# A graph kernel's second pass: four chunks by lists where three were, and where the dense entries, the own columns and the last product go

## The chip, the cores and the metric

The kernel runs on one core of a Trainium2 chip. The metric is the device time of one execution in microseconds (us). It was timed in 14 runs; the median counts.

## What is computed

A graph of 3327 nodes with 512 features goes through two layers. Both use the same sparse weighted adjacency matrix `adj`, given as a dense array. The density falls with the node number: the first nodes are neighbours of many, the last of few. Cut to what matters:

```python
# layer 0
h = maximum(layernorm(x), 0)
u = relu(adj @ (h @ W1) + b1)              # first pass over adj, 128 hidden features (u here is g in the kernel)
x = x + adj @ (u @ W2) + b2                # second pass over adj
# layer 1
h = maximum(layernorm(x), 0)
type_sum = adj @ h
attn_a = sigmoid([type_sum, h] @ Wa.T + ba); attn_b = sigmoid([type_sum, h] @ Wb.T + bb)
s = h @ W_sa;  scores = (s @ a_left)[:, None] + (s @ a_right)[None, :]
e = where(adj != 0, exp(-leaky_relu(scores, 0.01)), 0)
x_a = (e / (e.sum(1) + 1e-5)) @ s
x_b = adj @ (h @ W_gcnb) + b_gcnb
x = x + sigmoid(attn_a * x_a + attn_b * x_b)
```

## The kernel before

The nodes are padded to 3328, 26 blocks of 128 (`NB`). Chunks are four blocks wide (512 columns), the last to be visited two. `adjT` is the transposed adjacency matrix in DRAM. Five engines work side by side: TensorE (PE), VectorE (DVE), ScalarE (ACT), GpSimd (POOL) and SyncE (SP); each runs its own instructions in order, and SP, ACT and POOL also issue DMAs in that order.

**First pass** (lines 603 to 651). The loop `for n, c in enumerate(back)` visits the chunks from the last nodes to the first (`back`: columns 2816, 2304, 1792, 1280, 256, 768, 0). For each of the 26 row blocks j it multiplies u[j] by a 128x512 piece of `adjT` (L622), and DVE takes the largest magnitude of every group of 32 columns (L629, tile `most`). The loads of two row blocks each (512 KB, `load_adj`, L301) go through SP's queue into six buffers. From `most`, `make_lists` (L482) finds for each block of nodes and each pair of 32-node groups which rows have a nonzero in the group, and writes row numbers to `row_h` and `row_a`. The room for such a list is `list_rooms(NB)`: 8 entries of 64 rows each for block 1, falling to 3, and 2 for some. Where a block stands in `OWN`, its own columns are left out of the lists and kept dense; where it also stands in `TOP`, the first 64 nodes are too. `extra[i]` counts these dense entries (0, 1 or 2).

The tile `ae[i]` holds for block i the `adjT` pieces of all its entries, listed or dense. Listed pieces come by indirect DMAs of POOL, one for 128 rows, in the order of `gather_adj` (L187): some behind the matmuls of the first pass, some in the second, the rest in attention. Dense pieces come by `load_own` (L210): two loads of 64 rows per entry (16 KB each). They are issued on ACT from n = 2 on, at j = 6, 10, 16, 19 and 22, one block each time, and each waits for the matmul of that step (`pace`). ACT's queue also carries the loads of the hub columns `a_hub` and of weights (L334 to L347).

**Second pass** (lines 693 to 966). Of the seven chunks the first three of `back` (`LISTED = 3`, blocks 14 to 25) are summed by lists: POOL gathers rows of g from DRAM (`gather_g`, 68 of them, a ring of 24), and `list_sums` (L865) multiplies them by `ae` pieces of 64x32 (L882). The dense entries use g itself, or `g_top`, a copy of the first 64 rows of g (L908 to L913). The chunk's sums are copied by ACT, turned by PE (L897) and copied again. The other chunks (blocks 0 to 13: three of 512 columns, one of 256) are summed densely by `dense_sums` (L916), which reads `adjT` again (L925). What PE does when is written out in `PLAN`: `d` is one step of a dense sum, `s` one block of list sums, `t` the turn of a listed chunk, `x` a row block of layer 0's output and its normalization (`make_row`: L723 on PE, then DVE and ACT, a store to `h_dram`), `l` the turn of left scores, `h` one addition to the hub's sums (L775), `e` a block of hub scores on DVE and ACT. `MADE` is the order in which dense (d) and listed (l) chunks are finished. Every 1.4 us of estimated work (`SPACE`, `STEP`) POOL issues one gather, of g as long as the ring has room, otherwise the next of `gather_adj`.

"Hub" is block 0, whose 128 nodes have the most neighbours. It is summed densely: 26 additions of `a_hub` and 26 of `e_hub`. What PLAN leaves of them is done after the last row.

**Attention** (lines 1032 to 1330). Blocks 25 down to 1, each with `rooms + extra` entries, cut into segments of four or five at most. For each segment `attend` gathers the rows of h that the lists name (POOL, tiles `rows` and `hr`) and makes the scores; `sums` multiplies (L1135: eight instructions per entry); two blocks later `turn` and `weigh` multiply the sums by the weights (L1149, L1189, L1197) and `finish` makes the output. Dense entries use `h_own`, loaded for each block, or `h_top`, a copy of the first 64 rows of h in the memory of `a_hub`. After each block `fetch_ae` issues two more gathers of `ae`; what a block still lacks is fetched before its h rows. `LEAD` holds POOL back: the gathers of block i wait for the sums of block i+4 (i+3 for the first).

At the end block 1's product `p_a` is made in two column pieces in one PSUM bank, `cuts = (0, WH, D)`, so that the work on the first may begin early.

## Time and profile before

| | us |
|---|---|
| median of 14 runs | 792.63 |
| lowest and highest | 787.24 and 800.37 |
| the profiled execution | 791.12 |
| its span, first to last instruction | 789.4 |
| end of the first pass, first dense matmul of the second | 230.6 |
| last row's matmul (px) ends | 400.6 |
| POOL's first gather of h rows | 413.65 |
| attention's PE work without larger gaps from | 446.9 |
| last p_a matmul ends | 780.0 |

The page gives busy time by engine, forty slices, the DMA queues, the chain of work that ended last, and groups of instructions with count, busy time, mean duration and the idle time ahead of them. Times on timelines count from the span's start. A matmul of float32 is two PE instructions. Matmul records overlap, so the time of one comes from the distance between starts or from the group's busy time, not from its mean. "issue" is time in which the engine waited for nothing that the profile shows.

| queue or issue | count | size |
|---|---|---|
| a<-in_adjT_dram, SP | 129 | 512 KB |
| ae<-in_adjT_dram, ACT (own columns) | 52 | 16 KB |
| ae gathers, POOL | 178 | one of 128 rows |
| g_row gathers, POOL | 68 | |
| h row gathers, POOL (rows, hr) | 178 | |

### The profile page before, as it was taken

What the parts mean: (1) busy time and instruction counts of PE and PEld (TensorE: products, weight loads), DVE (VectorE), ACT (ScalarE), POOL (GpSimd) and SP (SyncE); (2) the same over time, 40 slices, a digit from 0 to 9 for tenths busy, and PEclk for the clock granted to TensorE, in tenths of its full rate; (3) what the DMA queues carried; (4) which work ended last, traced back from release to release, by engine and by line L of the source; (5) the groups of instructions that cost most, each with busy time, mean ns of one, the idle gap of its engine ahead of it and who ended that gap; (6) DMA issues with size and microseconds to landing.
All of it is one profiled execution on the core that took longest, in us unless ns stands there. A gap on an engine that the chain in (4) does not pass through costs nothing.

```text
span 789.4 us, 11919 instructions
## 1 busy us (share of the span) xinstructions
PE 715.9 (91%) x3715; PEld 389.2 (49%) x3715; DVE 484.3 (61%) x1530; ACT 204.7 (26%) x492; POOL 456.1 (58%) x487
## 2 busy tenths in 40 slices
PE   9999959998889989898797399889999999999994
PEld 7775424444454444344444165445555545555553
DVE  6777958889961337456282277347657475766552
ACT  7771000000000324445170123123132222222211
POOL 2400566766766767677607667776767776675300
PEclk9999979999999999999988799989999999999998
DMA  8789959999869999974249566756666777786500
GB/s 277 245 302 302 298 171 311 296 282 284 269 202 299 366 371 344 320 248 148 61 181 307 151 179 205 231 156 189 213 196 191 211 213 229 227 252 199 159 32 31
DMA packets 105738, 180.47 MB, mean 229 GB/s; under 512 B 21217, under 2 KB 38017, under 8 KB 105666
## 3 DMA queue, kind: packets, MB, share of 16 engines
q1 hardware_dynamic: 63632, 111.91, 42.0%
q0 software_dynamic: 22112, 54.46, 24.3%
q10 hardware_dynamic: 19922, 13.25, 5.4%
q8 instruction: 31, 0.51, 0.3%
q14 instruction: 41, 0.34, 0.1%
HBM read 157.64 MB, written 22.26 MB: 228 GB/s over the span
## 4 chain that ended last, share of the span: by engine, by line
PE 73%; issue 9%; DVE 5%; POOL 4%; DMA 3%; another core or an unknown queue 3%; ACT 1%; SPq 0%; ACTq 0%; POOLq 0%
PE acc_u L622 16%; PE acc L1135 11%; PE p_b L1189 10%; PE acc_g L925 9%; PE p_a L1197 9%; PE acc_hub L775 5%; PE px L723 3%; PE pu L380 3%; PE ptt L1149 2%; POOL hr L180 2%; DVE most L629 2%; PE acc_s L882 1%; PE pt L372 1%; POOL ae L180 1%
## 5 line engine op out<-in xcount | busy, mean ns | idle before, releaser
L180 POOL DMA_INDIRECT ae<-in_adjT_dram,row_a x178 | 186.1, 1046 | 130.3 <-DVE jb L578 57.4
L622 PE MATMUL acc_u<-a,rows 128*128 128x512 f32 (+1 forms) x364 | 160.2, 581 | 2.7 <-issue 2.7
L180 POOL DMA_INDIRECT hr<-h_rows,row_h x114 | 118.5, 1039 | 51.9 <-issue 28.0
L1189 PE MATMUL p_b<-W_g_sb,tyT 128*128 128x257 f32 x416 | 100.9, 391 | 10.4 <-issue 9.5
L629 DVE TENSOR_REDUCE most<-a 128x32 f32<-128x1024 f32 (+1 forms) x104 | 103.7, 1009 | 10.4 <-DMA a<-in_adjT_dram 6.8
L180 POOL DMA_INDIRECT rows<-h_rows,row_h x64 | 67.5, 1055 | 55.8 <-DVE es_hub L830 21.3
L1189 PEld LDWEIGHTS p_b<-W_g_sb,tyT 128*128 128x128 f32 x416 | 77.6, 192 | 43.1 <-issue 18.7
L622 PEld LDWEIGHTS acc_u<-a,rows 128*128 128x128 f32 x364 | 68.0, 197 | 61.7 <-issue 59.1
L1197 PE MATMUL p_a<-W_sa_sb,tyT 128*128 128x512 f32 (+2 forms) x216 | 94.4, 577 | 1.1 <-issue 1.0
L180 POOL DMA_INDIRECT g_row<-g_rows,row_h x68 | 71.6, 1053 | 29.9 <-issue 18.0
L925 PE MATMUL acc_g<-a,g 128*128 128x512 f32 (+1 forms) x208 | 85.3, 552 | 1.1 <-DMA a<-in_adjT_dram 1.1
L1164 DVE COPY tyT<-ptt 128x512 f32<-128x512 f32 x51 | 35.0, 686 | 69.4 <-PE ptt L1149 44.3
L1197 PEld LDWEIGHTS p_a<-W_sa_sb,tyT 128*128 128x128 f32 x216 | 40.6, 189 | 40.5 <-issue 38.7
L925 PEld LDWEIGHTS acc_g<-a,g 128*128 128x128 f32 x208 | 39.1, 194 | 39.3 <-issue 36.2
L1135 PE MATMUL acc<-hr,ae 64*64 64x512 f32 x456 | 54.7, 592 | 0.3 <-issue 0.3
L727 DVE SCALAR_TENSOR_TENSOR xb<-px,xb 128x512 f32<-128x512 f32 x26 | 17.9, 687 | 50.3 <-PE px L723 40.9
L390 ACT ACTIVATE gT<-acc_u,b_col 128x512 f32<-128x512 f32 (+1 forms) x7 | 4.6, 656 | 163.1 <-DMA ae<-in_adjT_dram 89.4
L988 DVE SCALAR_TENSOR_TENSOR a_hub<-h_own,w_own 128x512 f32<-128x512 f32 x52 | 35.5, 683 | 9.1 <-DMA rows<-h_rows,row_h 9.0
L278 DVE SCALAR_TENSOR_TENSOR ae<-ae 128x192 f32<-128x192 f32 (+2 forms) x31 | 12.2, 404 | 41.8 <-ACT ae L277 24.3
L1071 ACT COPY s_left<-pl 64x64 f32<-64x64 f32 x42 | 8.7, 206 | 106.7 <-PE pl L1067 52.6
L1135 PEld LDWEIGHTS acc<-hr,ae 64*64 64x64 f32 x456 | 19.1, 135 | 30.3 <-issue 28.8
L1149 PEld LDWEIGHTS ptt<-ident,ty 128*128 128x128 f32 x208 | 24.9, 144 | 18.0 <-issue 12.9
(166 smaller groups left out, 994.5 us busy)
## 6 DMA issues: line engine op xcount, KB each, us to landing
a<-in_adjT_dram SPq DMA_DIRECT2D x129, 512.0 KB
h_rows<-rows SPq DMA_DIRECT2D x26, 260.0 KB
h_own<-h_rows SPq DMA_DIRECT2D x26, 260.0 KB
x<-in_x_dram SPq DMA_DIRECT2D x26, 256.0 KB
xb<-in_x_dram SPq DMA_DIRECT2D x26, 256.0 KB
x<-xb ACTq DMA_DIRECT2D x26, 256.0 KB
x1b<-x SPq DMA_DIRECT2D x26, 256.0 KB
out_dram<-va SPq DMA_DIRECT2D x25, 256.0 KB
```

What stands on the lines that cost most here:

```text
L180: return nc.gpsimd.indirect_dma_start(out=dst, out_offset=None, in_=table, in_offset=bass.IndirectOffsetOnAxis(ap=rows, axis=0), bounds_ch ...
L380: nc.tensor.matmul(pu[:, :HID], hT[:, k, :], W1_sb[:, k, :], start=(k == 0), stop=(k == KD - 1))
L622: added = nc.tensor.matmul(acc[:, :w], u[j], a[:, :w], start=(j == 0), stop=(j == NB - 1))
L629: nc.vector.tensor_reduce(most[:, : w // GW, j : j + both], tiles.rearrange("p k (b i) -> p b k i", i=GW), axis=AX.X, op=ALU.max, apply_ab ...
L775: return nc.tensor.matmul(acc_hub[k], s, made_row(i)[:, :D], start=(n == 0), stop=(n == NB - 1))
L925: on_pe[0] = nc.tensor.matmul(acc[:, :w], g[j], a[:, n % per, :], start=(n == 0), stop=(n == NB - 1))
L988: nc.vector.scalar_tensor_tensor(junk, h[:, :D], 1.0, w_own[:, s, :], op0=ALU.mult, op1=ALU.mult, accum_out=node[i][:, 1 + s : 2 + s],)
L1135: added = nc.tensor.matmul(taken[i]["acc"][h][q * HALF : (q + 1) * HALF, :], both[half_p, q * n + k, :], taken[i][k0][k][half_p, q, :D], s ...
L1149: moved = nc.tensor.transpose(pt[:, k * P : (k + 1) * P], ty[h][:, k * P : (k + 1) * P], ident)
L1164: last = nc.vector.tensor_copy(dst, src)
L1189: last = nc.tensor.matmul(p_b[n][:, :WH], tyT[:, k, 0, :], W_g_sb[:, k, n * WH : (n + 1) * WH], start=(k == 0), stop=(k == KD - 1),)
L1197: last = nc.tensor.matmul(p_a[:, c0:c1], tyT[:, k, 1, :], W_sa_sb[:, k, c0:c1], start=(k == 0), stop=(k == KD - 1),)
```

## The change

- `LISTED` goes from 3 to 4: blocks 10 to 13 are summed by lists in the second pass. The dense chunks that stay are columns 0, 512 and 1024 (256 wide). `MADE` and `PLAN` are written anew; PLAN's hub steps go from 32 to 43.
- A list batch holds 16 columns (`LIST_W`) where it held 18 (`CW // NT`); `most` has one buffer where it had two.
- Four blocks (`NEXT`: 7, 8, 20, 22) get a third dense entry, nodes 64 to 127, and are in `TOP` and `OWN`. Their rooms go from 4 or 3 to 3 or 2. `g_top` and `h_top` become two tiles each.
- The own columns are loaded on SP's queue, one load at every odd j from n = 1 on, behind the dense loads and without a wait for a matmul.
- The last p_a has three pieces (0, 257, 448, 512), each in a bank of its own.

```diff
-LISTED = 3
+LISTED = 4
+LIST_W = 16
-MADE = "dldldld"
+MADE = "dldldll"
 PLAN = """
-d26 s1 d2 x1 d1 x1 d3 s1 x1 l1 d3 x1 e2 s1 d8 s1 d3 t1 d3 x1 s1 x1 e2 d7 x1 s1 d3 x1 e2 d4 s1
-d1 x1 d3 l1 x1 e2 s1 d3 t1 x1 h2 s1 d1 x1 e1 h2 d2 x1 h1 s1 h1 x1 e2 h2 d4 x1 s1 h2 x1 e2 h2
-d3 s1 d1 x1 h1 t1 h1 x1 e2 h2 d7 x1 h2 d2 x1 e2 h2 d8 x1 h2 d2 x1 e2 h2 d4 x1 h2 x1 h2 x1 h2
-x1 h2
+d24 s1 d4 x1 d1 x1 d1 s1 d2 x1 l1 d1 s1 d1 x1 e2 d6 s1 d2 t1 d2 x1 d1 x1 e2 d1 s1 d5 x1 h2 s1
+d1 x1 e2 h2 d1 s1 d5 x1 h2 l1 x1 e2 s1 h2 t1 d4 x1 s1 h2 x1 e2 h2 d7 x1 s1 h2 x1 e2 h2 d4 s1 d2
+x1 h2 d2 x1 e2 h2 s1 d1 h1 t1 h1 x1 h3 x1 e2 s1 h4 x1 s1 x1 e2 h4 x1 s1 x1 e2 h4 s1 t1 e1 x2 h3
+x1 h3 x1
 """
-TOP = 3, 4, 5, 9, 10, 11, 21, 24
-OWN = TOP + (1, 6, 7, 8, 12, 13, 14, 15, 17, 18)
+NEXT = 7, 8, 20, 22
+TOP = NEXT + (3, 4, 5, 9, 10, 11, 21, 24)
+OWN = TOP + (1, 6, 12, 13, 14, 15, 17, 18)
 def list_rooms(n_blocks):
-    rooms = [0, 8, 7, 5, 4, 4, 4, 4, 4] + n_blocks * [3]
-    rooms[21] = rooms[24] = 2
+    rooms = [0, 8, 7, 5, 4, 4, 4, 3, 3] + n_blocks * [3]
+    for i in 20, 21, 22, 24:
+        rooms[i] = 2
...
-    extra = [int(i in OWN) + int(i in TOP) for i in range(NB)]
+    extra = [int(i in OWN) + int(i in TOP) + int(i in NEXT) for i in range(NB)]
...
-    def load_own(i, load):
+    def load_own(i):
...
-                rows = slice(0, HALF) if k else cols
-                load(
+                rows = slice((k - 1) * HALF, k * HALF) if k else cols
+                nc.sync.dma_start(
                     ae[i][h * HALF : (h + 1) * HALF, k : k + n + 1 : n, :GW],
                     adjT[rows, cols].rearrange("j (q i) -> j q i", i=GW),
                 )
+                yield
...
-            if n > 1 and j in (6, 10, 16, 19, 22):
-                for i in own_order:
-                    load_own(i, load)
-                    break
+            if j % 2:
+                next(own_loads, None)
...
-                            nc.vector.memset(flag[:HALF, groups, 0:1], 0.0)
+                            covered = (extra[c0 // P + b] - 1) * HALF
+                            nc.vector.memset(flag[:covered, groups, 0:1], 0.0)
...
-                    if not batches or sum(rooms[k] for k, _ in batches[-1]) + rooms[i] > CW // NT:
+                    if not batches or sum(rooms[k] for k, _ in batches[-1]) + rooms[i] > LIST_W:
...
-                                        t = g_top if kk else g[i]
+                                        t = g_tops[kk - 1] if kk else g[i]
...
-        g_top = ae[1][:, : HID // GW, GW:]
-        for h in range(2):
+        g_tops = [ae[1][:, k * HID // GW : (k + 1) * HID // GW, GW:] for k in range(2)]
+        for k, t in enumerate(g_tops):
+            for h in range(2):
...
-                    h = h_top if k else h_own[i]
+                    h = h_tops[k0 + k - 1] if k0 + k else h_own[i]
...
-            p_a = bank(psB, f"p_a_{i}")
+            p_a = [bank(psA if n else psB, f"p_a_{i}_{n}") for n in range(len(cuts) - 1)]
...
-        h_top, junk, w_left = (free_hub[:, k * ROW : k * ROW + w] for k, w in enumerate((ROW, D, D)))
-        for h in range(2):
-            nc.sync.dma_start(h_top[h * HALF : (h + 1) * HALF, :], h_dram[:HALF, :])
+        *h_tops, junk, w_left = (
+            free_hub[:, k * ROW : k * ROW + w] for k, w in enumerate((ROW, ROW, D, D))
+        )
+        for k, t in enumerate(h_tops):
+            for h in range(2):
+                nc.sync.dma_start(
+                    t[h * HALF : (h + 1) * HALF, :], h_dram[k * HALF : (k + 1) * HALF, :]
+                )
...
-        weigh(1, turn(1, ty, True)[0], taken[1]["es"], (0, WH, D), True)[2]()
+        weigh(1, turn(1, ty, True)[0], taken[1]["es"], (0, WH, D - HALF, D), True)[2]()
```

More of the change, by code (lines that the diff above doesn't have):

```diff
@@ L329, in load_weights @@
                 load(W2_sb, W2)
-        own_order = iter([
-            i for c0, w in back for i in range(c0 // P, (c0 + w) // P) if i in OWN
-        ])
+        own_loads = iter(
+            None
+            for c0, w in back
+            for i in range(c0 // P, (c0 + w) // P)
+            if i in OWN
+            for _ in load_own(i)
+        )
         def load_behind(added, n, j):
@@ L550, in make_lists @@
                 f0 = first[batch[0][0]] + batch[0][1] * rooms[batch[0][0]]
-                at = l0p.tile([P, CW // NT, 2, HALF], BF16, tag="at", name=f"at_{f0}")
+                at = l0p.tile([P, LIST_W, 2, HALF], BF16, tag="at", name=f"at_{f0}")
                 for i, q in batch:
@@ L571, in make_lists @@
                 yield
-                past = l0p.tile([P, CW // NT, NB], BF16, tag="past", name=f"past_{f0}", bufs=1)
+                past = l0p.tile([P, LIST_W, NB], BF16, tag="past", name=f"past_{f0}", bufs=1)
                 nc.vector.tensor_tensor(
@@ L576, in make_lists @@
                 )
-                jb = l0p.tile([P, CW // NT], F32, tag="jb", name=f"jb_{f0}")
+                jb = l0p.tile([P, LIST_W], F32, tag="jb", name=f"jb_{f0}")
                 nc.vector.tensor_reduce(jb[:, :m], past[:, :m, :], axis=AX.X, op=ALU.add)
@@ L606 @@
             per = 2 * CW // w
-            most = l0p.tile([P, MG, NB], F32, tag="most", name=f"most_{c0}")
+            most = l0p.tile([P, MG, NB], F32, tag="most", name=f"most_{c0}", bufs=1)
             for j in range(NB):
@@ L651 @@
             next(lists)
-        assert next(own_order, None) is None
+        for _ in own_loads:
+            pass
         for s in range(2):
@@ L906 @@
         hubs = add_hubs()
-        g_top = ae[1][:, : HID // GW, GW:]
-        for h in range(2):
-            nc.scalar.dma_start(
-                g_top[h * HALF : (h + 1) * HALF],
-                g_dram[:HALF, :].rearrange("j (k f) -> j k f", f=GW),
-            )
+        g_tops = [ae[1][:, k * HID // GW : (k + 1) * HID // GW, GW:] for k in range(2)]
+        for k, t in enumerate(g_tops):
+            for h in range(2):
+                nc.scalar.dma_start(
+                    t[h * HALF : (h + 1) * HALF],
+                    g_dram[k * HALF : (k + 1) * HALF, :].rearrange("j (k f) -> j k f", f=GW),
+                )
         order = [i for c0, w in back for i in range(c0 // P, (c0 + w) // P)]
@@ L1021, in finish @@
         va = pool.tile([P, D], F32, tag="va", name=f"va_{i}")
-        for c0, c1 in zip(cuts, cuts[1:]):
+        for p, c0, c1 in zip(p_a, cuts, cuts[1:]):
             a, b = va[:, c0:c1], vb[:, c0:c1]
-            read_a = nc.scalar.activation(a, p_a[:, c0:c1], AF.Copy, scale=f[:, 0:1])
+            read_a = nc.scalar.activation(a, p[:, : c1 - c0], AF.Copy, scale=f[:, 0:1])
             nc.vector.scalar_tensor_tensor(b, b, r[:, 2:3], a, op0=ALU.mult, op1=ALU.add)
@@ L1192, in weigh @@
                     )
-            p_a = bank(psB, f"p_a_{i}")
+            p_a = [bank(psA if n else psB, f"p_a_{i}_{n}") for n in range(len(cuts) - 1)]
             with queued(between(last) if between else None):
-                for c0, c1 in zip(cuts, cuts[1:]):
+                for p, c0, c1 in zip(p_a, cuts, cuts[1:]):
                     for k in range(KD):
                         last = nc.tensor.matmul(
-                            p_a[:, c0:c1], tyT[:, k, 1, :], W_sa_sb[:, k, c0:c1],
+                            p[:, : c1 - c0], tyT[:, k, 1, :], W_sa_sb[:, k, c0:c1],
                             start=(k == 0), stop=(k == KD - 1),
@@ L1229 @@
         free_hub = a_hub.rearrange("p j i -> p (j i)")
[L1230 to L1232 removed]
+        *h_tops, junk, w_left = (
+            free_hub[:, k * ROW : k * ROW + w] for k, w in enumerate((ROW, ROW, D, D))
+        )
+        for k, t in enumerate(h_tops):
+            for h in range(2):
+                nc.sync.dma_start(
+                    t[h * HALF : (h + 1) * HALF, :], h_dram[k * HALF : (k + 1) * HALF, :]
+                )
         nc.sync.dma_start(w_left, w_dram[0, :].partition_broadcast(P))
@@ L1466 @@
                             )
-                    finish(l1w, i, p_a, p_b, p_s[:, 0:1])
+                    finish(l1w, i, [p_a], p_b, p_s[:, 0:1])
 def kernel(**inputs):
```

## The prediction

> **What bounds the kernel now.** I read the totals first, then a table of busy time by stage, then the chain that ended last, then the timelines of the places that the change touches.
>
> The totals put TensorE (PE) on top, in four of five microseconds of the chain too. That is an average, so the table by stage follows. Its columns are the stretch, then for PE, weight loads, VectorE (DVE), ScalarE (ACT) and GpSimd (POOL) the busy time and instructions, then the granted clock, the DMA engines' share and GB/s. I cut it at the end of the first chunk, at the second pass's first dense matmul (230.6), where the DMA share falls (347), at the last row's matmul (400.6), where attention runs without a break (446.9), and at PE's end.
>
> ```profile
> span 789.4 us, 11919 instructions
> PE 715.9 (91%) x3715; PEld 389.2 (49%) x3715; DVE 484.3 (61%) x1530; ACT 204.7 (26%) x492; POOL 456.1 (58%) x487
> 65.90:230.60 164.70, 147.06 (x677) 72.24 (x677) 135.98 (x313) 3.44 (x5) 99.69 (x97) 0.95 0.85 269
> 230.60:347.00 116.40, 108.25 (x567) 49.52 (x570) 52.33 (x181) 37.68 (x94) 82.27 (x79) 0.97 0.97 324
> 347.00:400.60 53.60, 45.00 (x164) 23.89 (x154) 27.94 (x95) 20.89 (x54) 33.75 (x33) 0.90 0.40 130
> 400.60:446.90 46.30, 28.11 (x92) 14.02 (x91) 20.60 (x79) 12.66 (x33) 23.76 (x24) 0.85 0.68 226
> 446.90:780.00 333.10, 323.08 (x1835) 180.22 (x1835) 197.50 (x700) 80.99 (x196) 204.21 (x194) 0.98 0.62 187
> ```
>
> The reader should see three regimes. In 230.6 to 347 the DMA engines are full (0.97) and PE is nearly so: two limits at once. In 400.6 to 446.9 PE works 28 of 46 us: a latency chain. From 446.9 on PE is the bound, 323 of 333 us. The prices come from these groups (count, busy us, mean ns of one) and pieces of the chain (start, us, what):
>
> ```profile
> L925 PE MATMUL acc_g<-a,g 128*128 128x512 f32 x156 | 73.0, 609 | 1.1 <-DMA a<-in_adjT_dram 1.1
> L882 PE MATMUL acc_s<-g_row,ae 64*32 64x128 f32 x272 | 10.5, 271 | 2.1 <-issue 2.1
> 322.64 3.26 issue
> 330.83 1.01 PE acc_s L882 x32
> 333.75 1.72 PE acc_hub L775 x4
> 659.54 4.45 PE acc L1135 x40
> ```
>
> Two instructions make one matmul. So a dense step of 512 columns costs 73.0/78 = 0.94 us (0.86 where they run back to back), one list instruction 1.01/32 = 0.032, a hub addition 1.72/2 = 0.86, and one list entry k of attention (8 instructions) 4.45 x 8/40 = 0.89.
>
> **The change, part by part.**
>
> *Second pass, PE up to the last row.* Blocks 10 to 13 leave the dense chunks: 26 steps of 512 columns go, -26 x 0.86 = -22.4 (-24.4 at 0.94). List instructions go from 336 (42 entries: 34 gathered, 8 own or top, x 2 x 2 x 2) to 512 (88 gathered slots x 4, 12 own, 6 first-half, 2 second-half entries x 8): +176 x 0.032 = +5.6, and one more set of four turning matmuls, +0.5. The new PLAN has 43 hub steps for 32, all ahead of the last x where two came behind it: 13 x 0.86 = +11.2. Those additions were made before in the latency stretch after 400.6, where they cost little, so here they are a real loss. Sum -5.1 to -7.1; I take -6.
>
> *Second pass, DMA.* 13 loads of 512 KB go, 6.8 MB, at the stage's 324 GB/s 21 us of full DMA; 20 more g_row gathers of 64 KB give back 4. Laying PLAN's steps out at the prices above, the 13th row's matmul should come 91 us after the first dense one and comes 106 after: 15 us are lost, mostly in the full DMA stretch. The new plan still has 73 of its 78 dense steps before that row, so most of the density remains. Between 0 and -15 I take -5, nearer the end that the unchanged density speaks for.
>
> *Round trips.* A listed chunk turns its sums: PE, ACT copy, PE, ACT copy, PE. The 3.26 above is PE standing before such a turn although three dense steps lay between; the three turns together cost 6.2. A fourth adds 2.1 like them, and the last one (PLAN's "s1 t1 e1 x2") has no cover, when the last sums and the copy are 4.3 to 5.7 us apart in the timeline. Against that the last dense chunk's own wait for its copy (5.5, before 394.93) has no counterpart at the end. Net +3, from -2 to +11.
>
> *Rows at the end.* In the timeline the last rows' matmuls queue up behind one another: the last one ends at 400.6 and its row is normalized at 409.6, 9.0 us, where an undisturbed row needs 4.0 to 5.3. The new plan spaces the last three by three hub steps, so the queue should drain: -4 (0 to -5). The stores on SyncE (SP), then W_g, then h_own, then POOL's first h gather all follow the last row:
>
> ```profile
> 396.79 13.86 SPq L686 DMA_DIRECT2D h_rows<-rows  x6
> 410.74 0.39 SPq L976 DMA_DIRECT2D W_g_sb<-in_W_gcnb_dram  x1
> 414.57 2.48 SPq L1051 DMA_DIRECT2D h_own<-h_rows  x3
> 425.73 5.64 PE L1189 MATMUL p_b<-W_g_sb,tyT 128*128 128x257 f32 x16 [5.82 <-issue]
> ```
>
> So what is saved ahead of the last row is saved whole. But SP now issues two more loads of 130 KB for the second h_top ahead of h_own, on which own_scores waits, and DVE's copy of tyT for block 0's p_b stands behind that: two issues of about 0.6 and no more cover: +1.2 (0.5 to 2).
>
> The fence's last line has PE idle 5.8 us and the half clock after it: 16 p_b instructions take 5.64, against 3.67 for others, so a cold start costs 2 us. PE will now idle there longer, with 11 hub additions fewer to fill it, but the start is cold already: no charge. The Trainium skill's page "TensorE: Matmul & The Clock Gate" (section "Why this matters for your kernels") asks for no PE gap over about 3 us, and so speaks against moving cover away from here. If the rule bit at two new places, each at the 2 us of this row, the sum would be 4 us worse.
>
> *First pass.* 52 own-column loads of 16 KB on ACT become 72 on SP, unpaced, one at each odd step behind the dense loads. On ACT each takes 0.62 to issue. 72 x 0.62 = 45 us of SP in 165, where SP waited 72 us for PE to release buffers: that wait covers it. If the cover were gone, each of 78 loads could be up to 0.65 late, +10 at most when nothing is prefetched; six buffers hold 10 us of work. The 20 more cost 2 us of DMA at the packets' 0.013 us. On the good side, chunks with own loads took 25.6 to 28.2 us and the one without 24.0, and SP's waits name an ae load of ACT once (2.3 us). I take 0, from -8 to +4. Lists of 16 columns for 18 make the same number of batches in every chunk, on a DVE with 29 us to spare: nothing.
>
> *Attention.* Blocks 7, 8, 20 and 22 lose a room and gain dense entries: 121 entries for 115, +6 x 0.89 = +5.3, all on the bound engine. Blocks 7 and 8 fall into two segments: some 1.5 us more each on DVE, which has 136 us of slack: nothing. The second pass takes 88 g gathers where it took 68, and so fetches 10 ae columns for 36; 57 ae gathers remain for attention where 39 did, and 170 h gathers for 178. That is +10 at POOL's period of 1.30, 13 us. POOL ran ahead of PE by 34 us at most blocks, 28 at block 2, 15 at block 1. The new order fetches 6 ae just before block 1 and 2 each from block 5 to 2, some 11 us later net, so PE still finds its rows: nothing, at most +5.
>
> *The end.* Today no read of p_a starts before its last matmul:
>
> ```profile
> 780.05 0.84 ACT L1024 ACTIVATE va<-p_a,f 128x257 f32<-128x257 f32 x2 [4.32 <-PE p_a L1197]
> 780.56 0.88 DVE L1025 SCALAR_TENSOR_TENSOR vb<-vb,r,va 128x257 f32<-128x257 f32 x2 [3.54 <-ACT va L1024]
> 781.99 0.82 SPq L1029 DMA_DIRECT2D out_dram<-va  x2
> ```
>
> With a bank for each piece, only 64 columns are left after the last matmul: from 780.05 to the last issue at 782.4 is 2.35 us, for 64 columns some 1.15. Eight narrow matmuls add 0.4. So -0.8 (-1.5 to +0.5).
>
> **Sum.** -6 - 5 + 3 - 4 + 1.2 + 0 + 5.3 - 0.8 = -6.3 us. The profiled execution took 791.12, with 1.7 around its span; that gives 784.8. It lies 1.5 below the median 792.63 of the runs shown, so for a median I say 786.
>
> **The rivals.**
>
> *A: the DMA bound gives all.* If the stretch to 347 is DMA's, the 6.8 MB less come off nearly whole: -15 in place of -5, total -16, 776. For it: DMA 0.97 and 15 us lost. Against: PE is 108 of 116 there too, and the rows and hub steps must still run. 0.18.
>
> *B: attention and the hub steps eat it.* If the last rows do not drain faster (0 for -4) and the DMA gives -3, the sum is -0.3, 792. For it: 16.5 us of PE work are put on the path in hub steps and entries. 0.10.
>
> *C, slower: PE stands at the uncovered turns.* At the top of the round trips, +11 for +3, with DMA's share at 0: +6.7, 799. It decides in the last 40 us before the last row, where the new plan runs five list blocks and two turns without a dense step between; it turns the sum once the waits at turns pass 15 us where they were 6.2. For it: 4.3 to 5.7 us each even with cover. Against: hub steps lie between most. 0.20.
>
> Forecast (about -6, 780 to 790): 0.52. Faster by over 0.3% (2.4 us, about what this measurement can tell) is forecast and A with little lost: 0.70. Within: 0.09, most of B. Slower: 0.21. The range runs from A to short of the top of C: 775 to 798.
>
> **What would show it.** Right: 52 L925 instructions of 512 columns fewer; last px 6 to 12 us earlier against the first dense matmul; row to relu under 6 at the end; L1135 at 968 instructions with 5 us more between 446.9 and the end; h gathers still over 5 us ahead at block 1. Wrong: waits before pt_s and px over 12 us in all (C); first-pass chunks longer than 28 us (SP); PE waiting for POOL in the last three blocks.

## The result, and the profile after

The changed kernel takes 822.74 us in the median of 10 runs (820.78 to 826.63), the kernel before 792.61 in 47: the ratio is 1.041 (95% interval 1.039 to 1.044). It is slower by 30 us where 6 us of gain were predicted. The profiled execution took 824.12, its span 822.4, so 33.0 more than the span before. That is read stage by stage:

| stage, us | before | after | difference | predicted |
|---|---|---|---|---|
| to the second pass's first dense matmul | 230.6 | 239.1 | +8.5 | 0 |
| from there to the last px | 170.0 | 173.7 | +3.7 | -8 |
| to block 24's sums, where attention runs without a break | 46.3 | 41.9 | -4.4 | -2.8 |
| attention, to the last p_a | 333.1 | 360.7 | +27.6 | +5.3 |
| to the end of the span | 9.4 | 7.0 | -2.4 | -0.8 |

The head of the page after, then its stages as before (stretch, PE, weight loads, DVE, ACT, POOL with instructions, granted clock, DMA share, GB/s):

```profile
span 822.4 us, 12249 instructions
...
PE 729.4 (89%) x3883; PEld 393.8 (48%) x3883; DVE 487.0 (59%) x1554; ACT 203.9 (25%) x497; POOL 459.7 (56%) x491
```

```profile
66.80:239.10 172.30, 149.57 (x664) 72.58 (x663) 136.05 (x322) 4.12 (x6) 100.06 (x97) 0.92 0.85 266
239.10:355.50 116.40, 104.50 (x610) 53.73 (x610) 51.01 (x175) 35.61 (x90) 81.70 (x78) 0.96 0.83 273
355.50:412.80 57.30, 46.71 (x264) 21.59 (x263) 33.08 (x117) 27.66 (x74) 28.11 (x27) 0.88 0.43 141
412.80:454.70 41.90, 17.80 (x70) 8.14 (x70) 15.09 (x57) 7.90 (x19) 23.84 (x24) 0.76 0.71 231
454.70:815.40 360.70, 348.07 (x1891) 189.75 (x1891) 202.41 (x719) 81.80 (x201) 213.14 (x204) 0.97 0.56 168
```

Two of the three regimes have changed. The full DMA of the second pass (0.97 before) is gone: 0.83 until the last dense matmul at 355.5. And yet no time came of it. In attention PE is "busy" 348 of 361 us, so it looks as bound by PE as before; but it does 1891 matmuls in that stretch for 1835, 3% more, in 8% more time. The groups show where (count, busy us, mean ns, idle time before):

```profile
L935 PE MATMUL acc_g<-a,g 128*128 128x512 f32 (+1 forms) x156 | 64.4, 552 | 2.4 <-issue 1.4
L1145 PE MATMUL acc<-rows,ae 64*64 64x512 f32 x256 | 51.1, 659 | 14.8 <-DVE vb L1030 9.1
...
L1145 PEld LDWEIGHTS acc<-rows,ae 64*64 64x64 f32 x256 | 15.3, 144 | 43.7 <-issue 33.6
```

The same 256 instructions on `rows` in the kernel before:

```profile
L1135 PE MATMUL acc<-rows,ae 64*64 64x512 f32 x256 | 32.5, 621 | 0.0
L1135 PEld LDWEIGHTS acc<-rows,ae 64*64 64x64 f32 x256 | 10.0, 138 | 17.0 <-issue 14.7 <-DMA hr<-h_rows,row_h 1.4 <-DMA rows<-h_rows,row_h 0.3
```

The dense sums keep their price: an instruction of 512 columns takes 609 ns in the mean in both kernels (the 552 above is mixed with narrower ones). But the weight loads of the 64-row sums on `rows` wait 43.7 us for 17.0, most of it for "issue", that is for nothing that the profile shows, and the same matmuls fill 51.1 us for 32.5. One place explains the view: block 4's sums, PE's timeline (start, us, what), and POOL's in the same 15 us.

```profile
735.40 1.09 PE L1145 MATMUL acc<-h_own,ae 64*64 64x512 f32 x8
736.31 1.04 PE L1145 MATMUL acc<-a_hub,ae 64*64 64x512 f32 x8
737.17 2.74 PE L1145 MATMUL acc<-rows,ae 64*64 64x512 f32 x21
740.08 0.62 PE L1145 MATMUL acc<-rows,ae 64*64 64x512 f32 x1 [0.17 <-issue]
741.49 0.59 PE L1145 MATMUL acc<-rows,ae 64*64 64x512 f32 x1 [0.78 <-issue]
742.88 4.68 PE L1145 MATMUL acc<-rows,ae 64*64 64x512 f32 x6 [0.81 <-issue]
747.83 2.57 PE L1145 MATMUL acc<-rows,ae 64*64 64x512 f32 x3 [0.27 <-issue]
```

```profile
736.59 1.00 POOL L184 DMA_INDIRECT ae<-in_adjT_dram,row_a  x1 [0.30 <-issue]
737.89 1.00 POOL L184 DMA_INDIRECT ae<-in_adjT_dram,row_a  x1 [0.30 <-issue]
...
746.10 1.00 POOL L184 DMA_INDIRECT ae<-in_adjT_dram,row_a  x1 [0.30 <-issue]
748.85 0.99 POOL L184 DMA_INDIRECT rows<-h_rows,row_h  x1 [1.75 <-PE acc L1145]
```

48 matmuls of 64 rows normally take 5.3 us. Here 37 run as usual until 739.9, and the last eleven take ten us: one pair of weight load and matmul each 0.70 or 1.40 us, though all their rows came 43 us earlier. In that time POOL issues the eight ae gathers that stand ahead of block 1's rows, back to back each 1.30 us. PE does not wait for POOL; it is slow while POOL gathers, and for the two or three us after. The clock does not explain it: the granted clock is 1.00 from 739.9 to 745.3, the spell's first five us, and 0.50 only from there on.

### The profile page after: what moved, and what is told of

Read it like the earlier page. It is cut to its first block, busy times and chain, and to the rows that moved or that the text cites. A ratio compares the mean times of both kernels' runs of the same rounds, so it can differ in the third digit from the quotient of the medians.

```text
span 822.4 us, 12249 instructions
## 1 busy us (share of the span) xinstructions
PE 729.4 (89%) x3883; PEld 393.8 (48%) x3883; DVE 487.0 (59%) x1554; ACT 203.9 (25%) x497; POOL 459.7 (56%) x491
## 4 chain that ended last, share of the span: by engine, by line
PE 81%; issue 7%; DMA 3%; DVE 3%; another core or an unknown queue 3%; ACT 1%; SPq 0%; POOL 0%; ACTq 0%; POOLq 0%; DVEq 0%
PE acc_u L630 17%; PE acc L1145 16%; PE p_b L1199 12%; PE p_a L1207 11%; PE acc_g L935 6%; PE acc_hub L784 5%; PE ptt L1159 3%; PE px L732 3%; PE pu L387 2%; PE acc_s L891 2%; DMA a<-in_adjT_dram 2%; PE p_list L575 1%; PE pt L379 1%; DMA hr<-h_rows,row_h 1%
## 5 line engine op out<-in xcount | busy, mean ns | idle before, releaser
L184 POOL DMA_INDIRECT ae<-in_adjT_dram,row_a x170 | 175.3, 1031 | 133.1 <-DVE jb L587 59.6
L630 PE MATMUL acc_u<-a,rows 128*128 128x512 f32 (+1 forms) x364 | 163.7, 588 | 6.5 <-issue 5.1
L184 POOL DMA_INDIRECT hr<-h_rows,row_h x106 | 110.7, 1044 | 49.6 <-issue 25.9
L184 POOL DMA_INDIRECT g_row<-g_rows,row_h x88 | 93.5, 1062 | 40.7 <-issue 21.7
L184 POOL DMA_INDIRECT rows<-h_rows,row_h x64 | 67.4, 1052 | 76.4 <-PE acc L1145 33.6
L1207 PE MATMUL p_a<-W_sa_sb,tyT 128*128 128x512 f32 (+3 forms) x224 | 93.9, 563 | 0.0
L935 PE MATMUL acc_g<-a,g 128*128 128x512 f32 (+1 forms) x156 | 64.4, 552 | 2.4 <-issue 1.4
L1145 PE MATMUL acc<-rows,ae 64*64 64x512 f32 x256 | 51.1, 659 | 14.8 <-DVE vb L1030 9.1
L935 PEld LDWEIGHTS acc_g<-a,g 128*128 128x128 f32 x156 | 30.5, 203 | 28.9 <-issue 25.4
L1145 PEld LDWEIGHTS acc<-rows,ae 64*64 64x64 f32 x256 | 15.3, 144 | 43.7 <-issue 33.6
```

What stands on the lines that cost most here:

```text
L184: return nc.gpsimd.indirect_dma_start(out=dst, out_offset=None, in_=table, in_offset=bass.IndirectOffsetOnAxis(ap=rows, axis=0), bounds_ch ...
L630: added = nc.tensor.matmul(acc[:, :w], u[j], a[:, :w], start=(j == 0), stop=(j == NB - 1))
L935: on_pe[0] = nc.tensor.matmul(acc[:, :w], g[j], a[:, n % per, :], start=(n == 0), stop=(n == NB - 1))
L1145: added = nc.tensor.matmul(taken[i]["acc"][h][q * HALF : (q + 1) * HALF, :], both[half_p, q * n + k, :], taken[i][k0][k][half_p, q, :D], s ...
L1207: last = nc.tensor.matmul(p[:, : c1 - c0], tyT[:, k, 1, :], W_sa_sb[:, k, c0:c1], start=(k == 0), stop=(k == KD - 1),)
```

## The experiments

Each kernel ran beside runs of the kernel before on the same chip; chips differ (the median of the kernel before was 791 to 807 where it ran several times), so ratios are compared, and times of stages only as they stand in profiles. "Attention" is the stretch of the table above, from block 24's sums to the last p_a. A block's "slot" is the time from the start of its sums to the start of the next block's, and a "spell" a time in which PE is slow as above.

### The parts of the change, one by one

**Own columns back on ACT** (in the changed kernel):

```diff
-                nc.sync.dma_start(
+                load(
                     ae[i][h * HALF : (h + 1) * HALF, k : k + n + 1 : n, :GW],
...
-            if j % 2:
-                next(own_loads, None)
+            if n > 1 and j in (6, 10, 16, 19, 22):
+                for i in own_order:
+                    load_own(i, load)
+                    break
```

> The changed kernel with its own columns back on ScalarE's queue, five blocks to a chunk as before. In the changed kernel the first pass ends 8.5 us later than before (239.1 against 230.6), and 27 us are lost in attention. If SyncE's own-column loads cost the first pass its time (theory O): first pass back near 231, the whole 814 to 816 us. If SyncE's waits cover them, as the prediction had it, and the first pass is late for another cause (theory L, the new order of chunks): still 237 to 240, the whole 821 to 824. Attention is the same by both, some 354 us from the first p_a to the last.

Measured: 1.041 (1.033 to 1.050), the same as the change; first pass 236.5, attention 360.2. **Own columns on SP alone** (in the kernel before, the same edit the other way):

> The kernel before with one part of the change alone: its 52 own-column loads on SyncE, one behind each odd dense step. Theory O (SyncE's loads are late for PE): first pass ends 4 to 8 us later than 230.6, the whole 797 to 800 us. Theory L or the prediction (SyncE's wait covers them): 228 to 232, the whole 790 to 794.

Measured: 1.012 (1.003 to 1.020), first pass 234.8, attention 336.6. So SP's loads are a small part: 0 to 2%. They do hold back the first chunk: the second one begins at 64.8 to 65.0 us in every profile with own columns on ACT and at 66.6 to 67.4 in every one with them on SP. In the changed kernel SP issues own loads at 27 to 36 us, and at 35 PE waits 1.3 us for its next `a`.

**Without the dense entries of blocks 7, 8, 20 and 22** (NEXT empty, rooms and OWN as before, the rest of the change kept):

```diff
-NEXT = 7, 8, 20, 22
+NEXT = ()
-OWN = TOP + (1, 6, 12, 13, 14, 15, 17, 18)
+OWN = TOP + (1, 6, 7, 8, 12, 13, 14, 15, 17, 18)
-    rooms = [0, 8, 7, 5, 4, 4, 4, 3, 3] + n_blocks * [3]
-    for i in 20, 21, 22, 24:
+    rooms = [0, 8, 7, 5, 4, 4, 4, 4, 4] + n_blocks * [3]
+    for i in 21, 24:
```

> The changed kernel with the dense entries of blocks 7, 8, 20 and 22 taken back: their rooms and own columns as before, nothing dense of nodes 64 to 127; the lists and the new plan stay. Attention then has 115 entries for 121 and the second pass 92 g gathers for 88. Theory F (PE stands in the sums of blocks 10 to 4 because POOL still fetches ae columns there, which the second pass no longer fetches): only the entries come back, about 5 us, so 815 to 819, with the sums of blocks 10 to 4 still 20 us too long. Theory E (it is the added dense entries that stall PE: the six more entries and what belongs to them): sums back to 0.89 us an entry, 792 to 798.

Measured: 1.060 (1.051 to 1.069), attention 385.0. **The new second pass alone** (the kernel before with LISTED, MADE, PLAN, LIST_W and the one buffer of `most` of the change):

> The kernel before with the second pass of the change alone: four listed chunks, the new order and plan; own columns on ScalarE, no dense entries of nodes 64 to 127, one bank for the last p_a. Theory F (fewer ae columns fetched in the second pass, so the fetches reach into the last blocks): still slow, 808 to 818, with stretched sums in the last blocks. Theory E or O (the loss belongs to the dense entries or the loads on SyncE): 786 to 794.

Measured: 1.070 (1.059 to 1.081), attention 379.9. Neither theory named times as long as these. The new second pass alone costs 7%, more than the whole change, and the dense entries, which the prediction charged with 5.3 us, give time back. What orders these kernels is the number of POOL gathers in attention: 217 before, 227 changed, 247 in these two.

### What a gather costs

From these traces a theory was made (R): when POOL gathers back to back for longer than some nine gathers, PE's issue slows. **Gathers that nothing uses**, added to the kernel before:

```diff
+            if i in (15, 12) and k0 == 0:
+                for d in range(9):
+                    with queued(gathered[0]):
+                        gathered[0] = gather(
+                            ae[1][:, (i == 12) * 9 + d, GW:], adj_groups,
+                            row_a[:, first[1] + d : first[1] + d + 1], NP * NG - 1,
+                        )
+                    if i == 12:
+                        pace(gathered[0], combined[-LEAD[1]])
```

> The kernel before, with two bursts of gathers that nothing reads added in attention (9 ae columns of block 1 each, into the half of its tile that is not yet in use): at block 15's turn without waits of their own, at block 12's turn each with a wait on a PE instruction that is long done. POOL's lead of 35 us covers both (12 us each), so by waits alone nothing is late. Theory R (a run of gathers back to back that goes beyond some 9 slows PE's issue to one pair of instructions in 0.7 us, of whatever kind the gathers are): PE stretched in the 10 to 15 us after the tenth gather of the run, 5 to 12 us lost at each burst, 800 to 815 us; if a met wait is enough to break a run, only at the first. Theory K (it is the late place of the fetches, or their blocks, that matters): no stretch at either, 790 to 794.

Measured, in one run: 828.0 against 795.7 for the kernel before, attention 363.9 (333.1). Both bursts cost: the slot of block 18 takes 26.7 us where it took 14.9, that of block 14 28.3 where it took 12.1. POOL's part of the second burst, and PE's timeline at block 14's sums (32 matmuls, normally 3.7 us):

```profile
581.55 0.99 POOL L180 DMA_INDIRECT ae<-in_adjT_dram,row_a  x1 [1.71 <-PE p_b L1198]
...
592.82 1.00 POOL L180 DMA_INDIRECT ae<-in_adjT_dram,row_a  x1 [0.30 <-issue]
594.12 1.00 POOL L180 DMA_INDIRECT hr<-h_rows,row_h  x1 [0.30 <-issue]
595.43 0.99 POOL L180 DMA_INDIRECT hr<-h_rows,row_h  x1 [0.30 <-issue]
```

```profile
600.22 3.88 PE L1144 MATMUL acc<-h_own,ae 64*64 64x512 f32 x8 [0.95 <-issue]
603.09 2.77 PE L1144 MATMUL acc<-rows,ae 64*64 64x512 f32 x4
606.62 2.60 PE L1144 MATMUL acc<-rows,ae 64*64 64x512 f32 x4 [0.76 <-issue]
609.43 1.86 PE L1144 MATMUL acc<-rows,ae 64*64 64x512 f32 x3 [0.20 <-DMA hr<-h_rows,row_h]
611.53 1.99 PE L1144 MATMUL acc<-rows,ae 64*64 64x512 f32 x3 [0.24 <-issue]
614.35 1.86 PE L1144 MATMUL acc<-rows,ae 64*64 64x512 f32 x2 [0.84 <-issue]
616.48 2.71 PE L1144 MATMUL acc<-rows,ae 64*64 64x512 f32 x8 [0.27 <-issue]
```

Nothing reads the columns of the burst, of the waits shown only 0.20 us is put down to rows, and PE needs 19 us for the 32 matmuls. The waits on a PE instruction long done, which the gathers of the second burst have, do not help: they make no pause, and 25 gathers follow one another with 0.3 us between them.

**Three ae columns a block** instead of two (`AE_PER = 3` in the changed kernel):

> The changed kernel with three ae columns fetched behind each block's gathers in place of two: all 57 are fetched by block 6, and the eight forced ones ahead of block 1 and three ahead of block 6 are gone. Theory K (late fetches cost PE): the sums of blocks 5 to 1 are clean, 800 to 808 us. Theory R (long runs): the 10 us of block 4 are gone, but the runs in the slots ahead become 9 and more, so that blocks 17 to 11, clean until now, lose some: 805 to 820.

Measured: 1.032 (1.028 to 1.036). Blocks 9 to 2 are clean, block 4 among them, but block 20 takes 23.9 us for 18.9, 19 21.6 for 18.9 and 14 20.2 for 12.0: the loss moved to where POOL now runs long, as R says.

**Gathers spread out**: each of attention's gathers waits for a PE instruction of its own, chosen at the like fraction of the slot three to four blocks ahead (two or three ae columns a block).

```diff
+        def spread():
+            if len(combined) >= 4:
+                lead = 3 + min(max(18 - slot["i"], 0), 8) / 8
+                at = len(pe_mark) - lead + min(slot["m"] / slot["n"], 0.95)
+                a = int(at)
+                t0, t1 = pe_time[pe_mark[a]], pe_time[pe_mark[a + 1]]
+                t = t0 + (t1 - t0) * (at - a)
+                done = max(k for k in range(len(pe_log)) if pe_time[k + 1] <= t + 0.01)
+                pace(gathered[0], pe_log[done])
+            slot["m"] += 1
...
-                    if k0 + k + q == extra[i] and len(combined) >= lead:
-                        pace(gathered[0], combined[-lead])
+                    spread()
```

> The changed kernel with every gather of attention paced behind a PE instruction of its own, spread evenly over a block's slot three to four blocks ahead, so that POOL never runs long without a break; two or three ae columns a block, none forced. Nothing is left out. Theory R: PE's stretched spells go, attention from first to last p_a falls from 354 to 325 to 332 us, the whole to 792 to 802. Theory K: the fetches are still there in the late blocks, so 810 to 822. If the density of gathers over 10 to 15 us counts and not the run, it lies between.

Measured: 1.025 (1.021 to 1.028), attention 350.3: ten us come back, less than half of what R hoped for, and the whole, 812.5, lies in the range that K named. Slots of nine or ten gathers still fill POOL's whole time. **The same in the kernel before**:

> The kernel before with the same pacing, two ae columns a block. Theory R: the spells at blocks 20 to 18 and 11 to 9 go, some 8 to 14 us, so 778 to 786 us. Theory K, or if gathers cost PE nothing before: 790 to 794.

Measured: 0.996 (0.993 to 0.999): the spell at blocks 20 and 19 is gone (11.2 and 11.7 us for 18.7 and 13.0), but attention is 333.1 as before, since smaller ones appear at 17, 15, 14 and 12 (13.4 to 15.0 us for some 12).

### Taking gathers away

**The changed kernel without its last 18 ae fetches**:

```diff
                     for k in range(max(k0, extra[i]), k1):
+                        if i == 1 or (i, q) == (6, 1) and k > 2:
+                            fetched[i] += 1
+                            continue
```

> The changed kernel with the last 18 ae fetches of attention left out (all 16 of block 1 and two of block 6), so that block 1's and a part of block 6's weights are not computed from the graph; 39 fetches remain in attention, as many as before, and every other instruction stays. Theory R (each gather beyond what POOL can issue with breaks costs PE about 1.5 us): attention from first to last p_a falls from 354 to 326 to 332 us, the whole to 794 to 801. If the loss belongs to PE's own work (six more entries, longer sums): 818 to 822.

Measured: 0.998 (0.994 to 1.002), attention 337.5. PE's timeline at block 4's sums, where the changed kernel needs fifteen us:

```profile
726.49 1.09 PE L1148 MATMUL acc<-h_own,ae 64*64 64x512 f32 x8
727.40 1.04 PE L1148 MATMUL acc<-a_hub,ae 64*64 64x512 f32 x8
728.26 3.61 PE L1148 MATMUL acc<-rows,ae 64*64 64x512 f32 x32
```

48 matmuls in 5.4 us. With these 18 gathers the whole loss of attention is gone but 4.4 us, and six entries at the predicted 0.89 are 5.3. This settles the main part. Even so the kernel is no faster than the one before: its first and second pass are as long as the changed kernel's (240.8 and 173.8 us).

**The dense entries and the three banks without the new second pass** (LISTED, MADE and PLAN of before, own columns on ACT):

> The change without its second pass and without the loads on SyncE: three listed chunks in the old order and plan, own columns on ScalarE, but the dense entries of blocks 7, 8, 20 and 22 and the three banks of the last p_a. Attention has 201 gathers where it had 217 and 121 entries where it had 115. Theory R: 16 gathers less are worth more than six entries, which cost 5 us; the spells of PE at blocks 20 to 18 and 11 to 8 shrink; 782 to 790 us. If gathers cost PE nothing: the entries alone, 795 to 798, less 1 to 2 for the end.

Measured: 1.001 (0.997 to 1.005), attention 338.7 with 197 gathers. A miss: attention is 5.6 us longer than before, about the price of the six entries, so in sum 20 gathers less give nothing back. Blocks 11 to 9 are 3.0 us shorter, but spells are left in attention's first blocks (24, 20 and 18), and 24 and 18 take 20.7 and 18.9 us for 17.6 and 14.9. **With the gathers spread**:

> The kernel of h3_next_banks with attention's gathers each paced behind a PE instruction, as in g3_spread_after, two ae columns a block. Theory R: runs of eight gathers with breaks between them everywhere, PE at 8.4 us a block and 0.89 an entry; 776 to 784 us. If spreading only moves POOL's work: the same as h3_next_banks.

Measured: 0.989 (0.984 to 0.993), attention 331.5. The spell at block 20 is gone, but with eight gathers a slot, spread out, blocks 18 and 15 still take 15.3 and 16.2 us for 12.0. **And with one or two ae columns a block in turn**, so 7 or 8 gathers a slot:

> The kernel of h4_next_banks_spread with one or two ae columns a block in turn instead of two, so that a block's slot of 12 us has 7 or 8 gathers. Theory R: the spells left at blocks 18, 15 and 14 (8 us in all) go as well, the ratio to the kernel before falls from 0.9885 to 0.975 to 0.985. If a spell comes by chance of place and not by rate: the same as h4.

Measured: 0.985 (0.979 to 0.991). It beats both kernels, by 1.5% and, against the change on the same chip (1.035), by some 5%. Its interval overlaps that of two columns a block, so it is not shown that seven or eight do better than eight.

### The second pass and the first

**Cover at the turns**:

```diff
-s1 h2 t1 d4 x1 s1
+s1 h2 d4 t1 x1 s1
...
-s1 d1 h1 t1 h1 x1 h3
+s1 d1 h4 t1 h1 x1
```

> The changed kernel with cover at two of the second pass's turns: the second turn comes after the four dense steps that followed it, the third after three more hub steps. In the changed kernel PE stands 5.1 and 6.1 us ahead of these two. Theory C (the copies of a turn are waited for without cover): 6 to 9 us less in the second pass, the last px 165 to 168 us after the first dense matmul where it was 173.7, the whole 813 to 816. If PE waits there for something else (the list matmuls before it end late): no change, 820 to 823.

Measured: 1.028 (1.022 to 1.033), but the second pass took 180.5, where the unchanged one on the same chip (in h1_no_last_ae) took 173.8. Against the changed kernel's profile the waits ahead of the turns halve, 14.3 to 7.0 us in all, and the list matmuls lose 8 us more. Theory C does not hold.

**Without the fourth chunk's g gathers**:

```diff
-                            yield first[i] + q * rooms[i] + k
+                            f = first[i] + q * rooms[i] + k
+                            yield None if (c0, w) == listed_chunks[3] else f
...
+                                    elif (c0, w) == listed_chunks[3]:
+                                        t = g[i]
```

> The changed kernel with the 24 gathers of g rows for the fourth listed chunk left out (its list matmuls take the block's own g rows instead, so the sums of blocks 10 to 13 are not the reference's); the places in the order where they stood stay empty. The changed kernel's second pass, from the first dense matmul to the last px, takes 173 to 176 us, with 88 gathers spread to 386. Theory R (the second pass too goes at the pace of its gathers, 1.5 us each): 24 fewer are worth 10 to 20 us there, 155 to 165. If the waits at the turns set it (theory C): 170 or more.

Measured: 1.011 (1.005 to 1.017). **The changed kernel once more, on the same chip**:

> The changed kernel as it is, once more, beside the others on one chip. By theory R the slow spells stand where POOL's gathers run without a break, so in the same places: blocks 20 and 19, 10 to 7 and 4, and the list matmuls of the second pass; the ratio 1.038 to 1.044. If the spells come by chance: other blocks.

Measured: 1.035 (1.029 to 1.042), attention 360.6 (360.7 the first time), with the spells at the same blocks: 25.0 us for block 4's slot (25.9), 18.1 at 19 (18.9), 17.3 at 8 (16.7). They belong to the program, not to chance. The second pass in the two runs, changed kernel first:

```profile
236.60:408.50 171.90, 149.57 (x873) 73.72 (x872) 83.41 (x288) 63.23 (x163) 109.14 (x104) 0.95 0.72 232
```

```profile
236.70:393.10 156.40, 145.50 (x873) 72.86 (x872) 82.85 (x288) 63.32 (x163) 84.67 (x80) 0.98 0.75 245
```

The same 873 matmuls in 156.4 us instead of 171.9, with 80 gathers instead of 104. The waits ahead of the turns fall from 16.2 to 3.5 us. So the waits belong to the gathers. The rows do not come too late: in the changed kernel's profile the last gather that a block's list sums need ended 12.6 to 26.5 us before the last matmul on it. Nor is it the copy's own length, 0.6 us. The chain of the first profile at the third turn:

```profile
365.16 0.38 PE acc_s L891 x2
...
366.63 1.87 PE acc_hub L784 x2
368.50 6.05 issue
374.56 1.12 PE pt_s L906 x4
```

ACT's copy of these sums waits for PE's signal, which comes at 373.89, eight us after the last list matmul in the trace, and starts at 373.92. From 368.5 to then PE and ACT stand while POOL gathers. Why the signal is late no run shows.

**Fewer gathers in the first pass** (kernel before, `if j % 2:` for `if j % 4 if w == CW else j % 2:`):

> The kernel before with gathers in the first pass behind every second dense step instead of three of four; those not fetched there are fetched later. Only the first pass is read. Theory R: with a gather in 1.7 us PE is not slowed there, the 36 us chunk falls to 24 to 27, the first pass ends at 215 to 224 instead of 230.6; the whole may be slower, as the gathers come back later. If the first pass's slow chunk has another cause (the lists' own work on VectorE, loads): 228 to 233.

Measured: the first pass from its second chunk on:

```profile
64.80:214.90 150.10, 142.48 (x680) 69.41 (x679) 136.05 (x313) 4.12 (x6) 70.19 (x70) 0.99 0.92 295
```

150.1 us, 214.9 at its end; the kernel before's first pass ended at 230.2 on the same chip (in h11_plain_sp). The chunk that takes 36 us takes 28.8. As a whole it is slower, 1.030 (1.022 to 1.036): 244 gathers are left for attention, which takes 376.2.

### What in a gather it is

**Plain transfers, and plain POOL work**, in the places of the bursts (kernel before; nine transfers on SP at block 15's turn, 16 memsets on POOL at block 12's):

> The kernel before, with what may make a gather cost PE taken apart, in the two places where g1_burst had its bursts: at block 15's turn nine plain transfers of the same shape (128 rows of 256 bytes) on SyncE's queue, whose descriptors POOL does not make; at block 12's turn some 10 us of POOL memsets and no transfer. If it is the transfers: PE stretched by 8 us or more at blocks 19 to 18. If it is POOL being busy without a break: at blocks 16 to 14. If it is POOL's making of descriptors for gathers alone: at neither, beside the spells that the kernel before has at blocks 20 to 18 and 11 to 9, and 790 to 800 us in all (SyncE's queue is 5 us later at block 15).

Measured, in one run each: 810.8 against 801.7. The transfers had no wait and were issued by 341 us, so that half says nothing. The memsets hold POOL from 571.96 to 578.29 without any spell of PE; but POOL is then late and issues gather after gather without a pause, and from the twelfth on, at 593.8, PE is slow: block 14's slot takes 18.1 us for 12.1. POOL stands nowhere for more than 0.5 us from 561.5 on (eight gathers, the memsets, then the gathers), so 32 us of unbroken work on POOL passed before PE became slow, where ahead of block 1 in the changed kernel (above) a run of twelve gathers, 14 us, was enough. So POOL's being busy does not suffice. **The transfers held in place by a wait**, 18 of them at block 13's turn:

```diff
+            if i == 13 and k0 == 0:
+                for d in range(18):
+                    with queued(gathered[0]):
+                        t = nc.sync.dma_start(
+                            ae[1][:, d, GW:], adjT[P : 2 * P, d * GW : (d + 1) * GW]
+                        )
+                        pace(t, combined[-LEAD[1]])
```

> The kernel before with 18 plain transfers of an ae column's shape (128 rows of 256 bytes) on SyncE's queue at block 13's turn, each with a wait on the PE instruction that block 13's gathers wait for, so that they start among them and not earlier. If the transfers of gathers are what slows PE: blocks 17 and 16, 12.0 and 11.2 us in the kernel before, grow by 8 us and more. If it is POOL's work on gathers: these two blocks keep their length, 12 and 11.2; SyncE's own work is some 9 us later there, which may delay a row's load by a few us at most.

SP's and POOL's instructions there, and PE's:

```profile
545.63 1.00 POOL L180 DMA_INDIRECT hr<-h_rows,row_h  x1 [0.30 <-issue]
...
546.20 9.32 SPq L1085 DMA_DIRECT2D ae<-in_adjT_dram  x18
...
553.47 1.00 POOL L180 DMA_INDIRECT ae<-in_adjT_dram,row_a  x1 [0.30 <-issue]
```

```profile
546.03 3.60 PE L1204 MATMUL p_a<-W_sa_sb,tyT 128*128 128x512 f32 x8
549.46 1.04 PE L1156 MATMUL ptt<-ident,ty 128*128 128x128 f32 x8
...
550.89 2.81 PE L1142 MATMUL acc<-hr,ae 64*64 64x512 f32 x24
553.62 3.73 PE L1196 MATMUL p_b<-W_g_sb,tyT 128*128 128x257 f32 x16
```

Measured, in one run each: 784.6 against 788.9; blocks 17 and 16 take 12.2 and 11.2 us (12.0 and 11.2), with 18 transfers of the gathers' shape among POOL's eight gathers. PE keeps its pace: 24 matmuls in 2.8 us. So plain transfers of this shape do not slow PE; the slowing belongs to gathers issued on POOL. Whether it is POOL's work on them or their indirect transfer, from POOL's own queue, these runs do not part.

## Why the prediction was wrong, point by point

**The step that failed** is the last of "Attention": it counted +10 gathers at 1.30 us, found POOL 34 us ahead of PE and 15 at block 1, and put "so PE still finds its rows: nothing, at most +5". PE did find its rows; POOL's lead at block 1 is 15.0 us still, and 35 to 48 from block 17 to 2. But a lead says when rows come, not what their gathering costs PE. Attention takes 27.6 us more, which is 22.3 beyond the price of the entries; that is the largest part of the 39.3 us between the forecast (-6.3) and the profile (+33.0). Where POOL has pauses, as in most slots of eight gathers in 12 us of both kernels, a gather costs nothing. The change has 18 more ae fetches and 8 fewer gathers of h; the fetches, five of them in a row ahead of block 6 and eight ahead of block 1, filled the pauses. The measured price is 1.3 to 1.7 us of PE for each gather above: 18 added cost 30.8 us (g1_burst), 18 left out give back 23.2 (h1_no_last_ae), and with 247 instead of 217 and the same 115 entries attention takes 46.8 to 51.9 more. By the change's own net ten it is 2.2, so where a gather falls counts too. POOL's 58% of the page hid it: that is an average too, with 1.00 us counted of each 1.30.

**PE work of the second pass**, -6: right. The stage's instructions of 512 columns fall from 269 to 242 and its list instructions rise from 336 to 512; at 0.43 and 0.032 us that is -11.6 and +5.6, and four more for the turn make it -5.6.

**DMA**, -5: none came, although the share fell: the 13th row's matmul, from whose lateness the term was read, comes 106.1 us after the first dense one for 106.4. (The new plan has 69 of its 78 dense steps before that row; the 73 of the prediction are the old plan's.) The changed kernel's second pass is held by its gathers: 104 in 155 us, 1.5 each, as in attention, and 24 fewer give 15.5 us (h8_skip_g). That they held the kernel before too, where the DMA engines were full, is likely by its 1.45 a gather but not shown.

**Round trips**, +3: PE stands 14.3 us ahead of the turns for 7.2 and 3.0 ahead of px for 7.3, +2.8 in all. Right in size by luck, as the reason is another (h5_cover, h8_skip_g). The list matmuls lose some 3 us more, which was not in the sum. The stage took 3.7 us more where -8 was forecast; with -5.6, +2.8 and +3 in place of the terms, 3.5 us are left. The granted clock is at half for 23.9 us of it where it was for 17.0, which by an estimate (half of 6.9) makes at most 3.5; the prediction named such a loss, 4 us, and left it out of its sum.

**Rows at the end**, -4: right. From the last row's matmul to its relu 4.75 us for 9.0; POOL's first h gather comes 8.9 us after the last px for 13.05. SP's chain there, as the prediction showed it before:

```profile
414.31 4.30 SPq L695 DMA_DIRECT2D h_rows<-rows  x4
418.70 0.38 SPq L986 DMA_DIRECT2D W_g_sb<-in_W_gcnb_dram  x1
...
422.55 2.40 SPq L1061 DMA_DIRECT2D h_own<-h_rows  x3
```

`h_own` is loaded 4 us sooner after the last row. The extra loads of `h_tops`, +1.2, are not seen: from the first h gather to block 24's sums it is 33.05 us for 33.25.

**First pass**, 0: +8.5 in the two profiles, and open. Without any change to it the first pass ended between 230.2 and 238.9 in profiles of the kernel before and of variants that differ only behind it. On one chip the change's ended 6 us later than that of before (236.6 for 230.2), on another not (236.2 and 237.0 for 234.5 to 238.9); and on a third the same changed first pass ended at 236.8 and at 240.8. Some 2 us are the first chunk's, with own columns on SP. What moves it most is the gathers again: 27 fewer take 15 us off (h9_first_half). The prediction's limit of 28 us for a chunk was passed twice beside the chunk of 36 (28.6 and 33.7); its reading before, 25.6 to 28.2 us for chunks with own loads, had left out that chunk of 36, in which own loads are issued too.

**Entries**, +5.3: right. Slots without a spell take 12.0 us with four entries, 12.9 with five, 13.7 with six.

**The end**, -0.8: right, 1.0. From the last p_a to the last issue it is 1.8 us (815.42 to 817.21) for 2.8; the other 1.4 us of the stage's -2.4 lie behind the last issue and were not forecast:

```profile
815.23 1.98 SPq L1039 DMA_DIRECT2D out_dram<-va  x3
815.42 0.31 ACT L1034 ACTIVATE va<-p_a,f 128x64 f32<-128x64 f32 x1 [0.38 <-PE p_a L1207]
```

**The rivals.** A had the DMA as the bound and fell with it. C named the right sign and the wrong cause: ahead of the last turn, the one without cover, PE stands 0.7 us, ahead of the second and third 5.1 and 6.1, and cover at these bought nothing. Its mark, over 12 us before pt_s and px, was reached (17.3), but by the same measure the kernel before had 14.5. A rival in which POOL's gathers cost PE without any wait was missing; the profile of before had its mark, the waits for "issue" at blocks 20 to 18, where block 20's slot takes 18.7 us for 11.2.

## What to carry to other kernels

Count the gathers of each stage against its time, not their lead or POOL's busy share: here eight in a row in a slot of 12 us, with a pause behind them, were mostly free, and each one above cost PE 1.3 to 2.2 us. A change that saves dense loads by lists pays in gathers, and those it pushes into a later stage are paid there; so a part's price needs the count of every stage behind it. When an engine is late for "issue", look at what another engine does without a pause at that moment, and test it with work that nothing uses.

## What the runs showed of the hardware

- In six traces (both kernels and the first four experiments), taken in steps of half a microsecond from 540 us to attention's last 60, PE's matmuls start 0.7 us apart or more in under 5% of the steps in which POOL is at the second to eighth gather of a run without a pause, in 14% at the ninth, in 56% at the tenth, and in 50 to 100% at each place behind it. It is no rule for every place: in POOL's pauses 21% of the steps are slow, and the list sums of the second pass, by the shortest time of a group of the same length, lose nothing with up to six gathers, 0.1 us in the mean with seven in the 12 us ahead of them, 0.3 with eight and 1.3 with nine.
- The gathers of h themselves land in time all along: the last packet of one comes 1.9 to 6.5 us after its instruction ends (both kernels and g1_burst). In a spell the instructions of PE often come 0.70 to 0.73 us or 1.40 apart, whatever they take otherwise: list sums (0.03), 64-row sums (0.11), p_b (0.23).
- The Trainium skill's page "DMA: Bandwidth & Descriptors" (section "SWDGE vs HWDGE vs iDMA") says that for transfers issued on POOL a program on its cores computes the descriptors, and that for those of SP and ACT hardware emits them. That is one difference between g1_burst, where 18 gathers cost 31 us, and h11_plain_sp, where 18 transfers cost none; that the gathers are indirect and the transfers plain is another. The section does not speak of PE, and how its issue comes to be slowed no run here shows.
- The page "Runtime: NRT & Kernel Launch" (section "Instruction fetch mechanics") has instruction fetch as mostly hidden. The spells look like a starved engine, but in both kernels' traces the 16 KB packets of the queue that holds PE's instructions come every 190 to 310 of PE's instructions, some 250 in the mean, in spells and out of them, and take 0.9 to 1.9 us each; so the trace does not show fetch to be late, nor rule it out.
